# Moving a plan into the last attention turn, early expert weights ahead of their rows, and one hidden layer into the other PSUM ring

## The chip, the cores and the metric

The kernel runs on one core of a Trainium2 chip. The metric is device microseconds (us) of one execution; nine runs were timed, and one more execution was profiled. The engines are PE (matrix multiply; PEld is its weight load), DVE (vector), ACT (scalar, activations), POOL (GpSimd) and SP, which here only issues DMAs. In the views of the profile, L12 is line 12 of the kernel, and times in a timeline count from the start of the span.

## The reference

The reference is a gated cross attention followed by a gated mixture of eight experts, in float32. B is 8, 256 tokens per batch entry, width 128, 16 heads of 64, 8 experts with a hidden width of 512.

```python
q = layernorm(x) @ Wq + bq ; k = ctx @ Wk + bk ; v = ctx @ Wv + bv      # ctx is 8 x 1601 x 128
scores = q k^T / 8, causal mask of 256 x 1601 (key j is seen by query i when j <= i), -1e30 where masked
x = x + tanh(g_xattn) * (softmax(scores) v @ Wo + bo)
y = layernorm(x)
expert of a token = argmax(softmax(y @ Wr + br))
for i in range(8):
    xi = y * (expert == i)
    out = out + (relu(xi @ W1[i] + b1[i]) @ W2[i] + b2[i])
x = x + tanh(g_ffn) * out
```

A token that an expert does not own still goes through it as zeros, so each token gets its own expert's output plus a constant of the other seven.

## The kernel before

**Attention.** Batch entries are taken in four pairs, heads in eight pairs. A group g is one pair of heads of one pair of batch entries: 32 groups (NG), g = 0 to 31; b is the batch entry in the pair, and turn index i = 2b + j with j the head. The loop over g is software-pipelined: in turn g, PE makes the queries and keys of group g + 1, the scores of group g, the transposes (`turn`) of the probabilities of group g - 2, and its product with the values. DVE takes the row maximum (`scores`, L549 and L551) and copies the transposes out of PSUM (L605); ACT takes the exponentials (`exps`, L572); DVE takes a reciprocal (L586), and POOL multiplies the probabilities with it (L595, two instructions for each b).

**Routing.** After a pair's attention output and second layer norm, `router(p)` makes logits and each token's expert, `router_places(p)` its place in a store of rows sorted by expert (14 small matmuls and five DVE steps), and `scatter(n)` on POOL's queue writes 128 tokens' rows there by an indirect DMA. Pair 3, the last, is handled in two halves `a` and `b` (`class Half`), straight after the loop.

**Early chunks.** A chunk is 128 rows of one expert. Those that pairs 0 to 2 fill completely are known early: `plan_full` (18 small DVE steps; L1054 is the line that records all of them) finds up to five, NA = 5, and writes their numbers to `load_full`. SP loads each number (`fetch_number`, L941), and issues DMAs of the chunk's rows (132 KB, `fetch_rows`, L945) and of its expert's weights (578 KB, `fetch_weights`, L955) from a copy in DRAM named `later`. Each early chunk is then transposed (`turned_rows`), goes through `first_layer`, `hidden`, `second_layer` and `sums` in `last_routing`, in between the routing of half `b`. The other 18 chunks follow in `experts`: first the eight own ones, whose rows can be fetched only when the last scatter has landed.

**What sets the order.** The schedule is manual: each engine runs its instructions in the order in which the program states them. The order around the change is `last_turns`, where g = 30 and l = 31. There DVE has, in order: reciprocal (31,0), copies of turns (30,0) and (30,1), reciprocal (31,1), nine plan steps, copies of (31,0) and (31,1), the other nine, copies of (30,2) and (30,3). On SP's queue, `fetch_full` follows the plan. PE goes on with products for pair 3's output (`y_last0`, `y_last1`, L779), the residual (L774), and the halves' routing.

**PSUM.** Of eight banks, four hold scores, two are the ring `pt` of the transposes, two the ring `misc`. A tile takes a bank of its ring where it is first written in program order, and waits for the readers of the tile that had it. `hidden_bank` gives an early first layer a bank of `pt`; the ring there goes xs_0, hs_0, xs_2, hs_1, hs_2, so hs_1 takes the bank of hs_0.

Of the kernel before, what the change touches and what calls it, by code (L numbers as in the profile page):

```python
# [35 lines left out]
NA = 5  # L36
# [17 lines left out]
def tile_gated_xattn_moe(  # L54
# [19 lines left out]
    def misc(name):  # L74
        return ps_m.tile([P, 512], F32, tag="misc", name=name)
# [226 lines left out]
    _, first = counted("first", [E], [[N, E]])  # L302
    _, fills = counted("fills", [E, NFULL], [[0, E], [P, NFULL]], P)
# [175 lines left out]
    NG = NC * NPAIR  # L479
# [459 lines left out]
    def fetch_number(i):  # L939
        plan, j = ("full", i) if i < NA + E else ("rest", i - NA - E)  # L940
        number[i] = nc.sync.value_load(chunk_of[plan][0:1, j : j + 1], min_val=0, max_val=E * NT - 1)  # L941
# [18 lines left out]
        engine.tensor_tensor(r[:, D : 2 * D], r[:, D : 2 * D], v[:, AT_C : AT_C + D], ALU.add)  # L960

    def hidden_bank(i):
        if i < NA:
            return ps_t.tile([P, 512], F32, tag="pt", name=f"hs_{i}").unsqueeze(1)
        return ps_s.tile([P, 2, 512], F32, tag=f"sc{i % 2}", name=f"hs_{i}")
# [68 lines left out]
        nc.gpsimd.memset(warm[:, 0:1], 0.0)  # L1034

    def fetch_full():
        weights_behind = {1: (0,), 4: (1, 2, 3, 4)}
        for i in range(NA):
            fetch_number(i)
            fetch_rows(i)  # L1040
            for k in weights_behind.get(i, ()):
                fetch_weights(k)

    def last_turns(a):


        g, l = NG - 2, NG - 1
        b = Half(1, misc("y_last1")[:, 0:S], banks[0][:, 1, 0:S], banks[1][:, 1])
        steps = plan_full()

        def plan(n):
            for _ in range(min(n, len(steps))):
                f, *args = steps.pop(0)
                f(*args)  # L1054

        normalized(l, 0)
        turn(g, 0)
        turn(g, 1)
        exps(l, 1)
        scatter(10)  # L1060
        normalized(l, 1)
        scatter(11)
        apart()
        a.residual()
        a.out(NC - 4)
        plan(9)
        turn(l, 0)
        turn(l, 1)
        a.attend(g, nc.scalar)
        plan(len(steps))  # L1070
        fetch_full()
        a.out(NC - 3)
        turn(g, 2)
        turn(g, 3)
        a.attend(l, nc.scalar)
        a.out(NC - 2)
        b.out(0)
        b.residual()
        a.out(NC - 1)
        a.statistics()  # L1080
        a.deviation()
        turn(l, 2)
        turn(l, 3)
        a.turned()
        b.out(1, 2)
        a.logits()
        b.attend(g, nc.vector)
        a.normalized()
        a.choice()
        b.out(3)  # L1090
        b.attend(l, nc.scalar)
        a.apply()
        b.out(4, 5)
        a.places(cb[NPAIR - 2], cb[NPAIR - 1])
        a.scatter(0)
        b.out(6, 7)
        return a, b
# [85 lines left out]
    def beside_scores(p, c):  # L1183

        f, n = p - 1, p + 1
        outs = []
        if f >= 0:
            if p < NPAIR - 1:
                outs = [c - 2] if 2 <= c <= 5 else []
            else:  # L1190
                outs = [2 * c - 4, 2 * c - 3] if 2 <= c <= 3 else []
            if outs:
                attention_out(f, outs)
                for t in range(max(outs[0] - len(outs), 0), outs[0]):
                    norm2_stats(f, t)
            if c == (7 if p < NPAIR - 1 else 5):
                norm2_turn(f)
        if n < NPAIR:
            if c == 3:
                prologue_c(n)  # L1200
            if c == 5:
                prologue_x(n)
        if outs:
            evict_out(f, outs)
            if outs[-1] == 3:
                for t in outs:
                    norm2_stats(f, t)
                ln_scales(f"y{f}")
        if f == 1 and c == 0:
            router(0)  # L1210
        if f == 1 and c == 1:
            router_places(0)
        if f == 2 and c == 0:
            router(1)
        if f == 2 and c == 1:
            router_places(1)
        if f == 2 and c == 6:
            router_places(2)

    def beside_values(p, c):  # L1220

# [6 lines left out]
    with tc.manual_schedule():  # L1228
        plain_constants()
        for t in range(4):  # L1230
            ln_stats("x0", x_sb[0], t)
        ln_scales("x0")
        keep_awake(22)
        bias_vectors()
        prologue_c(0)
        keep_awake(3)
        prologue_apply(0)
        prologue_x(0)
        keep_awake(3)
        query(0)  # L1240
        masks = [step for p in range(NPAIR) for step in [mask_bias(p)] * 4]
        mask_steps = lambda n: [next(masks.pop(0)) for _ in range(n)]
        mask_steps(4)
        key(0, nc.vector)
        value(0)
        value(1, nc.vector)
        biases(0)
        scores(0, 0)
        exps(0, 0)
        mask_steps(4)  # L1250
        scores(0, 1)
        routing_constants()
        mean, rest_of = mean_value(), others()
        for g in range(NG):
            p, c = g // NC, g % NC
            old, new = g - 2 if g >= 2 else None, g + 1 if g + 1 < NG else None
            if g == 1:
                gates()
            if NC + 3 <= g < 2 * NC + 3:
                for i in range(2 * (g - NC - 3) + 1, min(2 * (g - NC - 3) + 3, NFILL)):  # L1260
                    fill(i)
            if p >= 1 and c == 2:
                residual(p - 1)
            if old is not None:
                turn(old, 0)
            if new is not None:
                query(new)
            if g == NC + 1:
                next(mean)
            if old is not None:  # L1270
                turn(old, 1)
            if g == NG - 1:

                o_old = misc(f"o_{old}")
                a = Half(0, misc("y_last0")[:, 0:S], banks[0][:, 0, 0:S], banks[1][:, 0])
                a.out(*range(NC - 4))
            if g > 1:
                exps(g - 1, 1, 0)
            if g > 0:
                beside_copies(p, c)  # L1280
            if NC - 4 <= g < NC:
                mask_steps(2)
            if new is not None:
                key(new)
            if g > 1:
                exps(g - 1, 1, 1)
            if g == 0:
                exps(0, 1)
            if old is not None:
                turn(old, 2)  # L1290
            if 1 <= g <= NG:
                for b in range(2):
                    normalized(g - 1, b)
            if p + 1 < NPAIR and c == 3:
                ln_scales(f"x{p + 1}")
            if g in (1, 2, 3, 5, 6):

                add_keys(g if g < 4 else g - 1)
            if g == 6:
                experts_weights()  # L1300
            if p < NPAIR and c == 4:
                add_bo(p)
            if g == NC - 1:
                join_keys()
            if g in (20, 21, 22, 24):
                next(rest_of)
            if g + 2 < NG:
                value(g + 2)
            if g == NC + 1:
                next(mean)  # L1310
            beside_values(p, c)
            if old is not None:
                turn(old, 3)
            if g == 3:
                router_constants()
            if g == 2:
                scaled()
            beside_scores(p, c)
            if g == 0:
                beside_copies(p, c)  # L1320
            if g == 1:
                routing_casts()
                more_constants()
            if g > 0:
                biases(g)
                scores(g, 0)
                exps(g, 0)
                scores(g, 1)
            if g == NC:
                next(mean)  # L1330
            if old is not None:
                values(old, o_old if g == NG - 1 else None)
            if g == NG - 3:
                router(2)
            if g == 0:
                add_keys(g)
            if NC + 4 <= g < NC + 4 + E:
                other(g - NC - 4)
            if 21 <= g < 28:
                next(rest_of)  # L1340
            if g == NC + 12 + E:
                keep_weights()
            if 20 <= g < 24:
                scatter(g - 20)
            if g == NG - 2:
                residual(NPAIR - 1)
            if 26 <= g:
                scatter(g - 22)
        last_routing(*last_turns(a))
        experts()  # L1350


# [31 lines left out]
```

## Time and profile before

| | us |
|---|---|
| median of 9 runs (lowest, highest) | 358.85 (357.04, 359.51) |
| the profiled execution | 358.12 |
| its span | 356.4 |
| PE busy | 333.9 (94%) |
| DVE busy | 245.4 (69%) |
| POOL busy | 216.3 (61%) |
| ACT busy | 208.0 (58%) |
| mean granted TensorE clock | 0.990 |

The page's slices show where the time lies: the attention loop to some 285 us, the last routing and the early chunks to 315, the expert chunks to 348, and the last stores. Busy time of PE is no proof of work at full speed: a matmul at half clock counts double. The granted clock is 1.0 for nearly the whole span; the stretches where it is not are the ones to look up. In the timeline views the columns are: start, us, engine, line, operation, written<-read, shapes, count, and in brackets the engine's idle time before it with what ended it. In sums over stretches: length, then busy time of PE, PEld, DVE, ACT and POOL with counts, granted clock, share of DMA, GB/s.

### The profile page before, as it was taken

Reading aid. Unit: us, or ns where it says so; the run is one execution under the profiler, and the core shown is the slowest. Engines: PE = TensorE matmul, PEld = TensorE weight load, DVE = VectorE, ACT = ScalarE, POOL = GpSimd, SP = SyncE. Lnnn points to the kernel's source line nnn. Section 1 sums busy time; section 2 is a strip of 40 time slices with the busy share of each in tenths; the row PEclk is TensorE's granted clock in tenths of the full one; section 3 lists DMA queues with packets and bytes.
Section 4 is the critical chain, followed back from the end, with each engine's and each line's share of the span. In section 5 each row is a group of like instructions: output and inputs, shape, how many; then the busy total and the mean of one; then the engine's idle time right before and its main releaser. Section 6 shows DMA issues by size and latency. Waiting matters only on the chain.

```text
span 356.4 us, 9265 instructions
## 1 busy us (share of the span) xinstructions
PE 333.9 (94%) x3244; PEld 236.1 (66%) x3244; DVE 245.4 (69%) x857; ACT 208.0 (58%) x743; POOL 216.3 (61%) x315
## 2 busy tenths in 40 slices
PE   7978999999999999999999999999999879889993
PEld 2435656667677766666766566677566657879993
DVE  3578889784777778787766887846787775654441
ACT  2277687765556757565565765745765712546651
POOL 6165675672365777769673566593775841717773
PEclk9999999999999999999999999999999989999997
DMA  6989775797899995000000000000390007659940
GB/s 206 275 140 202 116 107 86 110 325 220 235 386 383 386 384 184 2 2 2 3 2 15 17 18 16 2 2 15 151 404 30 30 32 230 234 161 345 399 152 16
DMA packets 36471, 53.69 MB, mean 151 GB/s; under 512 B 3945, under 2 KB 22973, under 8 KB 36424
## 3 DMA queue, kind: packets, MB, share of 16 engines
q1 hardware_dynamic: 28280, 44.00, 36.3%
q0 software_dynamic: 7360, 8.73, 12.9%
q8 instruction: 26, 0.43, 0.5%
q10 hardware_dynamic: 784, 0.36, 0.3%
q14 instruction: 21, 0.17, 0.1%
HBM read 27.82 MB, written 25.71 MB: 150 GB/s over the span
## 4 chain that ended last, share of the span: by engine, by line
PE 61%; DVE 14%; DMA 9%; ACT 6%; issue 3%; POOL 3%; ACTq 1%; SPq 1%; POOLq 0%; DVEq 0%
PE pt L603 8%; DMA rows<-in_ctx_dram 7%; PE k L491 7%; PE o L616 7%; PE y L660 6%; PE hs L986 6%; PE sc L541 5%; PE v L506 5%; PE ys L1002 5%; DVE sc L551 5%; PE q L484 4%; ACT prob L572 4%; PE y_last L779 2%; DVE nmax L549 2%; POOL prob L595 2%
## 5 line engine op out<-in xcount | busy, mean ns | idle before, releaser
L572 ACT ACTIVATE prob<-sc,nmax 128x129 f32<-128x129 f32 (+1 forms) x256 | 105.4, 426 | 89.1 <-DVE nmax L551 66.5
L595 POOL TENSOR_TENSOR prob<-prob,rs 128x256 f32<-128x256 f32 (+1 forms) x128 | 102.9, 863 | 60.2 <-DVE rs L586 58.7
L603 PEld LDWEIGHTS pt<-ident,prob 128*128 128x128 f32 x384 | 46.5, 141 | 55.4 <-issue 44.3
L605 DVE COPY probT<-pt 128x384 f32<-128x384 f32 x128 | 67.2, 545 | 11.7 <-PE pt L603 11.3
L603 PE MATMUL pt<-ident,prob 128*128 128x128 f32 x384 | 64.3, 278 | 3.8 <-DVE probT L605 2.2
L551 DVE CUSTOM_DVE_ANT_0 sc<-sc,bias 128x256 f32<-128x256 f32 x128 | 55.3, 432 | 4.5 <-DVE nmax L549 0.2
L572 ACT ACTIVATION_READ_ACCUMULATOR prob<-sc,nmax 128x1 f32 x256 | 53.7, 210 | 0.0
L616 PE MATMUL o<-probT,v 128*64 128x256 f32 x480 | 45.6, 332 | 0.0
L541 PE MATMUL sc<-kT,qT 64*64 64x256 f32 (+3 forms) x1024 | 41.9, 298 | 0.0
L616 PEld LDWEIGHTS o<-probT,v 128*64 128x64 f32 x480 | 29.7, 136 | 16.8 <-issue 7.0
L491 PE MATMUL k<-cT,arena 128*128 128x512 f32 x64 | 35.5, 636 | 2.6 <-DVE arena L634 1.6
L506 PE MATMUL v<-arena,cT 128*128 128x512 f32 x64 | 33.1, 601 | 1.7 <-ACT qT L486 1.6
L484 PE MATMUL q<-xT,arena 128*128 128x512 f32 x64 | 33.1, 598 | 0.1
L541 PEld LDWEIGHTS sc<-kT,qT 64*64 64x64 f32 x1024 | 31.6, 134 | 0.1
L549 DVE TENSOR_REDUCE nmax<-sc 128x2 f32<-128x258 f32 x64 | 26.9, 420 | 4.1 <-PE sc L541 3.8
L586 DVE RECIPROCAL rs<-ssum 128x4 f32<-128x4 f32 x64 | 11.1, 173 | 25.1 <-ACT prob L572 22.1
L1020 POOL DMA_INDIRECT out_dram<-o,rows x18 | 17.9, 996 | 15.7 <-DVE o L1013 11.5
L486 ACT ACTIVATE qT<-q,bqT 128x512 f32<-128x512 f32 x32 | 22.2, 694 | 7.8 <-PE q L484 7.3
L994 ACT ACTIVATE h<-hs,arena 128x128 f32<-128x128 f32 x60 | 17.1, 368 | 11.9 <-ACT h L994 9.7
L660 PE MATMUL y<-wo_sb,arena 128*128 128x128 f32 x192 | 23.3, 276 | 0.4 <-DVE zero L370 0.2
L497 ACT ACTIVATE kT<-k,bT 128x512 f32<-128x512 f32 x31 | 21.4, 692 | 2.5 <-PE k L491 2.2
L660 PEld LDWEIGHTS y<-wo_sb,arena 128*128 128x128 f32 x192 | 22.2, 192 | 0.9 <-DVE zero L370 0.9
(242 smaller groups left out, 506.7 us busy)
## 6 DMA issues: line engine op xcount, KB each, us to landing
store<-blank SPq DMA_DIRECT2D x16, 1056.0 KB, 14.7
arena<-later SPq DMA_DIRECT2D x15, 578.0 KB, 6.0
rows<-in_ctx_dram POOLq DMA_DIRECT2D x5, 1024.0 KB, 9.5
later<-ws SPq DMA_DIRECT2D x1, 4624.0 KB, 15.8
rows<-store SPq DMA_DIRECT2D x23, 132.0 KB, 2.3
ws<-in_L_ffn_W_dram SPq DMA_DIRECT2D x1, 2048.0 KB
ws<-in_L_ffn_W_dram SPq DMA_DIRECT2D x8, 256.0 KB, 3.7
rows<-in_ctx_dram SPq DMA_DIRECT2D x1, 1024.0 KB, 7.2
```

The costliest lines, as they stand in the source:

```text
L484: nc.tensor.matmul(ps, lhsT=wq_sb[:, c * P : (c + 1) * P], rhs=xT[p], start=True, stop=True)
L491: nc.tensor.matmul(ps, lhsT=wk_sb[:, c * P : (c + 1) * P], rhs=cT[p], start=True, stop=True)
L506: nc.tensor.matmul(ps, lhsT=cT[p][:, t * P : (t + 1) * P], rhs=wv_sb[:, c * P : c * P + 512], start=True, stop=True)
L541: nc.tensor.matmul(s[HB * u : HB * (u + 1), j, at : at + n], lhsT=q[r, lo : lo + HB], rhs=k[r, b * S : b * S + n], start=(t == 1), stop=True,)
L549: nc.vector.tensor_reduce(m[:, 0], s[:, :, U0:K1], AX.X, ALU.max, negate=True)
L551: nc.vector.tensor_tensor_reduce(out=s[:, j, K1:U1], in0=s[:, j, K1:U1], in1=bias[:, 2 * (g // NC) + b], scale=-1.0, scalar=-NEG_ALL, op0= ...
L572: nc.scalar.activation(pr[:, j, lo:hi], s[:, j, lo:hi], AF.Exp, bias=m[:, t, j : j + 1], scale=-1.0 if t else 1.0, accum_out=sm[:, t, j : ...
L595: nc.gpsimd.tensor_tensor(pr[:, :, lo:hi], pr[:, :, lo:hi], r, ALU.mult)
L603: nc.tensor.transpose(ps[:, n * P : (n + 1) * P], pr[:, j, K0 + n * P : K0 + (n + 1) * P], ident)
L605: nc.vector.tensor_copy(pt, ps[:, 0 : 3 * P])
L616: nc.tensor.matmul(o[DK * j : DK * (j + 1), n * P : S], lhsT=v[:, 2 * b + n, cols], rhs=probT[g, 2 * b + j][:, 0:S] if n == 0 else probT[g ...
L660: nc.tensor.matmul(ps[:, i * D : (i + 1) * D], lhsT=attT[p * NC + c][:, t * P : (t + 1) * P], rhs=wo_sb[:, c], start=(c == 0), stop=(c == ...
```

## The change

Five edits, made together:

- `router_places(2)` moves, in turn 30, from before the scores to after the values of group 28 (and so behind them on PE and DVE).
- `plan_full` is called in turn 31; its 18 steps are issued as 4 after turn (29,1), 3 after group 30's reciprocals, 3 in `last_turns` after reciprocal (31,0), and the last 8 before `fetch_full`.
- In `last_turns`, `normalized(l, 0)` moves behind `turn(g, 0)`, `turn(g, 1)` and `exps(l, 1)`.
- `fetch_full` issues the five numbers and weights first, and the five rows behind them.
- `hidden_bank(1)` takes a bank of `misc`.

```diff
     def hidden_bank(i):
+        if i == 1:
+            return misc("hs_1").unsqueeze(1)
         if i < NA:
             return ps_t.tile([P, 512], F32, tag="pt", name=f"hs_{i}").unsqueeze(1)
...
     def fetch_full():
-        weights_behind = {1: (0,), 4: (1, 2, 3, 4)}
+
         for i in range(NA):
             fetch_number(i)
+            fetch_weights(i)
+        for i in range(NA):
             fetch_rows(i)
-            for k in weights_behind.get(i, ()):
-                fetch_weights(k)
-
-    def last_turns(a):
+
+    def last_turns(a, plan):
...
-        steps = plan_full()
-
-        def plan(n):
-            for _ in range(min(n, len(steps))):
-                f, *args = steps.pop(0)
-                f(*args)
-
-        normalized(l, 0)
         turn(g, 0)
         turn(g, 1)
         exps(l, 1)
+        normalized(l, 0)
+        plan(3)
         scatter(10)
         normalized(l, 1)
         scatter(11)
         apart()
         a.residual()
         a.out(NC - 4)
-        plan(9)
         turn(l, 0)
         turn(l, 1)
         a.attend(g, nc.scalar)
-        plan(len(steps))
+        plan(18)
         fetch_full()
...
         if f == 2 and c == 1:
             router_places(1)
-        if f == 2 and c == 6:
-            router_places(2)
...
             if g == NG - 1:
+                full = plan_full()
+
+                def plan(n):
+                    for _ in range(min(n, len(full))):
+                        f, *args = full.pop(0)
+                        f(*args)
+
+                plan(4)
 
                 o_old = misc(f"o_{old}")
...
             if 1 <= g <= NG:
                 for b in range(2):
                     normalized(g - 1, b)
+            if g == NG - 1:
+                plan(3)
...
             if g == NG - 3:
                 router(2)
+            if g == NG - 2:
+                router_places(2)
...
-        last_routing(*last_turns(a))
+        last_routing(*last_turns(a, plan))
```

## The prediction

> **What bounds the kernel now.** I read the page first (PE busy 94% of the span), then the chain of waits through the last attention turns and the routing, then each engine's timeline there, SP's queue, and last the sums over the stretches of the granted clock. From 315.65 us on PE runs without a gap to 348 (the expert chunks), and the attention loop up to 270 us isn't touched. So the end moves by what moves the first own chunk, and the change is decided between 270 and 315 us.
>
> The chain of waits, start, us, what:
>
> ```profile
> 287.28 1.28 DVE wide_full L1054
> ...
> 289.23 0.48 DVE probT L605
> 289.70 0.04 issue
> 289.75 0.33 PE pt L603
> ...
> 305.96 1.16 PE hs L986 x8
> ...
> 312.81 2.02 DMA rows<-store
> ```
>
> The plan sits on the chain: copies of the last turns wait behind it on DVE, and PE behind the copies. Later the chain runs through the second early first layer to the own rows, which wait for the last scatter. The engines' timelines:
>
> ```profile
> 275.90 1.95 PE L779 MATMUL y_last<-wo_sb,arena 128*128 128x128 f32 x16
> 289.75 1.01 PE L603 MATMUL pt<-ident,prob 128*128 128x128 f32 x6 [1.82 <-DVE probT L605]
> 305.96 1.16 PE L986 MATMUL hs<-xsT,arena 128*128 128x128 f32 x8 [0.91 <-ACT h L994]
> ...
> 287.28 1.27 DVE L1054 TENSOR_TENSOR wide_full<-end_full,num_i 128x40 f32<-128x40 f32 x1
> 289.02 0.20 DVE L1054 TENSOR_TENSOR wide_full<-num_e,whose_full 128x40 f32<-128x40 f32 x1
> 286.87 1.61 POOL L595 TENSOR_TENSOR prob<-prob,rs 128x256 f32<-128x256 f32 x2
> 277.08 0.70 ACT L637 ACTIVATE arena<-o,bT 128x512 f32<-128x512 f32 x1
> ```
>
> To see: the same 128x40 step takes 0.20 us alone and 1.27 while POOL normalizes; it ends as POOL's second instruction does (288.48). SP's queue, and three granted-clock stretches (PE is the first busy column):
>
> ```profile
> 293.62 1.72 SPq L945 DMA_DIRECT2D rows<-store  x2
> 295.67 0.33 SPq L955 DMA_DIRECT2D arena<-later  x1
> 296.83 2.62 SPq L945 DMA_DIRECT2D rows<-store  x3
> 299.69 2.12 SPq L955 DMA_DIRECT2D arena<-later  x4
> ```
>
> ```profile
> 287.89:291.30 3.41, 1.59 (x15) 1.09 (x14) 3.13 (x13) 0.00 (x0) 1.74 (x3) 1.00 0.12 42
> 291.30:294.72 3.42, 3.42 (x18) 2.94 (x15) 1.34 (x5) 0.47 (x1) 0.00 (x0) 0.50 0.03 5
> 301.54:304.96 3.42, 2.69 (x21) 2.07 (x20) 1.45 (x10) 0.97 (x3) 2.29 (x5) 1.00 0.98 336
> ```
>
> After a stretch with 1.59 us of PE work the clock is 0.50 for the next 3.4 us; after one with 2.69 it isn't (nor after one with 1.76, early in the kernel).
>
> **Part 1: the third pair's places move behind group 30's scores.** Five DVE steps (273.06 to 273.98) leave the path ahead of the row maximum. That could start when its scores are done, 273.33 instead of 273.90 (at group 31 the maximum follows the scores' start by 0.83): 0.57 gained, and ACT's exponentials move with it: 275.48 to 274.91, the eviction L637 277.08 to 276.51, group 30's second exponentials end 278.83 instead of 279.40. The steps come back on DVE at 275.98 to 276.90 and PE's 14 small matmuls (0.43) after the values. The places' bank now comes after o_28's in the ring of two. In the trace y_last0 starts at 275.90, before L637 reads o_28 (277.08), so it stood in the places' bank; in the new order its turn is o_28's. I take that: a.out(0 to 3) waits for L637, 277.27. The other end: the places' bank, 276.95.
>
> **Part 2: plan in pieces.** Pitches are those of the plan's rows (18 steps from 286.02, less the held 1.05 and a pair of copies). DVE: copies of turns (29,0), (29,1) 276.90 to 277.90, plan(4) to 278.91. PE: a.out 277.27 to 279.06, turn (29,2), its copy 279.59 (before 278.22), reciprocals 280.06, and POOL's normalization of group 30 starts 0.33 later. plan(3): the reduce runs, wide_full is issued 0.5 after the reciprocal, inside POOL's first instruction (0.57 then 1.03 long), so I let it end with the second, as in the row shown: 282.05. Then one reduce, the copy of (29,3), and group 31's maximum starts at **282.8, before 280.31: 2.5 later**. Bounds: not held, 281.4; without the bank wait too, 280.8; held through all four of POOL's instructions, 284.3.
>
> From there by rows: both maxima 2.65; the two copies of group 30, now ahead of the reciprocal, 1.0; POOL's normalization 0.33 + 1.6, under which plan(3) is held at no cost but 0.3 (the next reciprocal waits for ACT anyway, 288.3); transposes and two copies of group 31, 1.47; then the first of the 8 steps left falls into POOL's next normalization (it starts 1.17 after the other's end, being behind scatter(10)) and ends with it, 2.77 after that end; the seven others 1.4. So load_full is ready 9.75 after the maximum: **292.55, before 291.79, 0.76 later**. Of 18 steps 10 leave the turn's end, and the gain goes into the wait for the maximum. PE does lose its 1.82 stall, but waits instead from 284.8 to 288.4 for the normalization; it would meet the slow clock one stretch earlier (as much work as before lies in it) and reach the early rows' turn at 301.7, as before (301.57).
>
> The Trainium skill speaks against this part: SBUF — State Buffer, "Who interferes with whom", says that a DVE instruction with two SBUF inputs contends with a GpSimd instruction that reads SBUF, and that the later one fully blocks until the first finishes. By that rule each hold ends with the instruction under way (287.50 in the trace), load_full is ready some 2 us earlier, and the sum would be 357.6. The row, which outlasts the next instruction too, decides.
>
> **Part 3: weights ahead of rows.** Before, rows 0 and 1 were issued 1.83 and 3.17 after load_full and landed 2.1 later, with five us to spare. Now SP issues: load and weights 0 at +1.3 (1.83 less the rows' own waits), then 1.15 each (1.145 for number and row), rows from +6.5. The queue keeps order: rows issued behind weights at 324 to 334 us took 4.9 to 5.5 us to land, alone 2.1. A row's fixed part is 2.1 less its 135 KB at 365 GB/s (what the DMA moved from 321 to 335 us), 1.75. So row 1 lands at 1.3 + 1.75 + (5 x 592 + 2 x 135) KB / 365 GB/s = 11.9 after load_full: **304.4**. (The same sum gives 307.9 for the last weights before; the trace has 308.0.) The early weights' gain is nothing: before, they were there before their layers. Behind the waiting transposes on PE stand the second half's transposes, its logits, first_layer(0): the path to the last scatter. From row 1 to the places' matmuls: 0.25 + 0.91 (transposes, ACT, to the logits) + 0.47 + 0.97 + 0.35 + 0.99 = 3.95, that is 308.4; before 306.95. So 1.4 later, with part 4 in it. DVE, POOL, the scatter's landing and the own rows keep their distance (306.95 to 314.96), PE's early chunks too (7.5 us to 314.47).
>
> PE then idles from 301.7 to 304.4. In the stretch 301.54 to 304.96 about 0.8 us of work is left, under the 1.59 that slowed it, so the clock is 0.50 to 308.4: of the 2.8 us of PE work ahead of the places the half lost is about 1.3. Sum: 1.4 + 1.3 = 2.7 later. The Trainium skill (TensorE: Matmul & The Clock Gate, "Why this matters for your kernels") puts the limit at gaps over some 3 us; by that rule this gap costs nothing and the sum is 1.4. The trace slowed after a 1.82 gap with thin work around it.
>
> **Part 4: hs_1 in the other ring.** y_last0 was read at 296, so the bank is free: the 0.91 wait for hidden(0) goes. ys_0 takes y_last1's bank, read by 302.7. Nothing is late; it's worth 0.9 at most, counted above.
>
> **Sum.** 358.1 (the profiled execution; span 356.4) + 2.7 = 360.8. The runs' median is 358.85, 0.7 above that execution, so I leave the sum as it is and let the range lean up.
>
> **Rivals.** (a) The rows come late but the clock doesn't drop: the stretches run free of the kernel's own order, and a boundary in the middle of the gap splits it. 359.5. For: 2.7 of 3.4 us; against: thin work on both sides. (b) Faster: POOL doesn't hold DVE, every moved step runs in its 0.2. Then the maximum is at 281.4, load_full at 281.4 + 2.65 + 1.0 + 1.95 + 1.45 + 1.55 = 290.0, row 1 at 301.9, PE waits 1.2 with no slow clock, the places come at 305.85: 1.1 earlier, **357.0**. It decides from load_full before 291.1 (306.95 - 15.85) on. For: big_full and tri_full, two inputs in SBUF, took 0.26 and 0.23 beside a scatter; against: wide_full at 1.27. (c) The hold ends an instruction sooner, or y_last0 keeps its bank with the slow clock missed: 357.4 to 359, within 0.3%. (d) The change doesn't do what it says: if rows overtook weights, they'd land near load_full + 9 and everything but parts 1 and 2 would vanish; the 5 us landings speak against it.
>
> **Chances.** The forecast 0.45 (its own range 359.9 to 361.8), (a) 0.15, (b) 0.17, (c) and (d) 0.23. A measurement tells 0.3% (1.1 us) from no change: faster 0.17, same 0.23, slower 0.60. The range runs from 357.3, a little over (b), to 362.3, the maximum held through all four instructions (1.5 more).
>
> **What would show it.** Right: y_last0 starts after L637; a 128x40 step of over 1 us just after group 30's reciprocals; group 31's maximum 2 to 2.5 later against group 30's scores; load_full at 292 to 293; xs waits 2 to 3 us for rows<-store, weights issued ahead; hs L986 has no wait for h; a clock of 0.50 in a stretch near 305. Wrong: load_full before 291, or xs not waiting.

## The result, and the profile after

| | before | after |
|---|---|---|
| median, us (runs) | 358.49 (46) | 363.53 (14) |
| lowest, highest | 356.42, 361.97 | 362.72, 365.87 |
| the profiled execution, us | 358.12 | 361.58 |
| its span, us | 356.4 | 359.9 |
| mean granted clock in it | 0.990 | 0.984 |

The ratio after to before is **1.0145, 95% interval 1.0126 to 1.0164**: 5 us slower. The forecast was 2.7 us slower, with a range that ended at 362.3. So the direction was right and the size was not.

Group 30's scores start at 272.75 us in the trace after and at 272.50 before; 0.25 is taken off where a time after is set against one before. Below, "the places" means the start of the last half's places matmuls (L716). The chain of waits after (start, us, what):

```profile
273.58 0.44 DVE nmax L549
...
280.79 0.62 DVE wide_full L1271
...
285.95 1.59 POOL prob L595 x2
287.58 1.33 PE pt L603 x5
...
299.31 5.53 DMA rows<-store
304.97 0.61 PE xs L979 x2
...
313.54 2.44 DMA store<-rows,posi_last
316.19 2.06 DMA rows<-store
```

The plan's long step is gone from the stretch where it stood, and what has come in is a transfer, the early chunks' rows, 5.53 us from their issue at 299.31 until PE can go on. The engines' timelines after show the wait and the plan's places:

```profile
277.53 2.05 PE L779 MATMUL y_last<-wo_sb,arena 128*128 128x128 f32 x16 [0.86 <-ACT arena L637]
286.59 0.33 PE L603 MATMUL pt<-ident,prob 128*128 128x128 f32 x1 [1.89 <-POOL prob L595]
304.97 0.61 PE L979 MATMUL xs<-ident,rows 128*128 128x128 f32 x2 [2.27 <-DMA rows<-store]
308.58 1.91 PE L988 MATMUL hs<-xsT,arena 128*128 128x128 f32 x8
310.29 0.24 PE L716 MATMUL sc<-hot_last,before 128*128 128x8 bf16 x2
...
280.79 0.61 DVE L1271 TENSOR_TENSOR wide_full<-end_full,num_i 128x40 f32<-128x40 f32 x1
282.01 0.42 DVE L549 TENSOR_REDUCE nmax<-sc 128x2 f32<-128x258 f32 x1
289.42 0.99 DVE L1271 TENSOR_TENSOR wide_full<-wide_full,end_full 128x40 f32<-128x40 f32 x1
291.74 0.17 DVE L1271 CAST load_full<-at_full 128x13 int32<-128x13 f32 x1
280.74 3.17 POOL L595 TENSOR_TENSOR prob<-prob,rs 128x256 f32<-128x256 f32 x4 [1.87 <-DVE rs L586]
```

xs is the transpose of the early rows. It waits 2.27 us on PE, and the last half's places, behind it, come at 310.29 where they came at 306.95. load_full, the early chunks' numbers, is ready at 291.91, 0.1 earlier than before once the 0.25 is taken off. SP's queue after, and the stretches of the granted clock (the columns as before):

```profile
293.26 5.70 SPq L955 DMA_DIRECT2D arena<-later  x5
299.31 3.01 SPq L945 DMA_DIRECT2D rows<-store  x5
```

```profile
286.98:290.39 3.41, 2.81 (x14) 1.77 (x14) 2.17 (x4) 0.53 (x3) 3.18 (x4) 0.50 0.13 43
290.39:293.81 3.42, 3.42 (x17) 2.71 (x18) 2.44 (x10) 0.47 (x1) 1.14 (x2) 0.50 0.11 41
...
304.05:307.46 3.41, 2.01 (x14) 1.64 (x15) 1.34 (x7) 0.38 (x1) 3.12 (x8) 1.00 0.59 206
307.46:310.87 3.41, 3.41 (x22) 3.35 (x22) 1.42 (x7) 2.23 (x8) 0.29 (x1) 0.50 0.09 32
310.87:314.29 3.42, 3.42 (x32) 3.42 (x32) 2.45 (x13) 1.95 (x8) 1.86 (x3) 1.00 0.11 40
```

All five weights are issued ahead of the rows. The clock is 0.50 in the stretch behind the gap, and in two stretches behind the 1.89 us wait for POOL as well; before it was 0.50 in one stretch of this part.

### The profile page after: what moved, and what is told of

Its sections match the earlier page's. It is cut to its first block, busy times and chain, and to the rows that moved or that the text cites. A ratio compares the mean times of both kernels' runs of the same rounds, so it can differ in the third digit from the quotient of the medians.

```text
span 359.9 us, 9261 instructions
## 1 busy us (share of the span) xinstructions
PE 337.8 (94%) x3244; PEld 238.5 (66%) x3244; DVE 246.3 (68%) x857; ACT 207.9 (58%) x743; POOL 216.3 (60%) x315
## 4 chain that ended last, share of the span: by engine, by line
PE 61%; DVE 17%; ACT 7%; DMA 6%; issue 4%; POOL 3%; SPq 1%; POOLq 0%; DVEq 0%; ACTq 0%
PE pt L603 8%; PE k L491 8%; PE o L616 6%; DVE sc L551 6%; PE v L506 6%; PE y L660 6%; PE sc L541 5%; ACT prob L572 5%; PE hs L988 4%; PE q L484 4%; PE ys L1004 4%; DVE nmax L549 2%; DMA rows<-store 2%; DVE arena L634 2%; PE sc L522 2%
## 5 line engine op out<-in xcount | busy, mean ns | idle before, releaser
L603 PEld LDWEIGHTS pt<-ident,prob 128*128 128x128 f32 x384 | 47.6, 143 | 54.0 <-issue 44.0
L603 PE MATMUL pt<-ident,prob 128*128 128x128 f32 x384 | 65.3, 282 | 2.9 <-POOL prob L595 2.6
```

Of the source, the lines that this page charges most:

```text
L603: nc.tensor.transpose(ps[:, n * P : (n + 1) * P], pr[:, j, K0 + n * P : K0 + (n + 1) * P], ident)
```

## The experiments

The theory after the result: the whole loss is part 3 (weights ahead of rows), through rows that land late and a clock that drops in the wait for them. Its rivals: the plan in pieces (parts 1 and 2) costs something too, or the lateness alone, without the clock, makes the loss.

Each timed run lists its mean granted clock. In the stretches of the traces the clock is 1.0 or 0.50, so the time that a run spent at half clock is 2 x span x (1 - clock). That view of the runs is used further down.

**Undo part 3 alone.** The changed kernel with the old order on SP's queue:

```diff
     def fetch_full():
-
+        weights_behind = {1: (0,), 4: (1, 2, 3, 4)}
         for i in range(NA):
             fetch_number(i)
-            fetch_weights(i)
-        for i in range(NA):
             fetch_rows(i)
+            for k in weights_behind.get(i, ()):
+                fetch_weights(k)
```

> The changed kernel with the early rows issued as before (rows 0 and 1, weights 0, rows 2 to 4, weights 1 to 4); the plan in pieces and hs_1 stay. Late-rows theory (rows behind 2.96 MB of weights keep PE waiting, then a slow clock): the wait of xs for rows<-store goes, PE comes to it some 0.75 us later than before because of the plan, hs_1 gives back up to 0.9, so about the time of the kernel before, 357.5 to 359.5. Rival (the plan's pieces hold group 31's maximum and slow the clock for two stretches, and that is the loss): 361.5 to 363.5, nearly all of it stays.

Measured: 0.9998 [0.9963, 1.0034], 358.85 us against 358.87. xs waits for nothing, and the places come 33.17 us after the start of group 30's scores (34.45 before, 37.54 after). Without part 3 nothing is lost.

**Part 3 alone**, the reverse edit made in the kernel before:

> The kernel before with one part alone: five numbers and weights issued ahead of five rows. Late-rows theory: xs waits till about load_full + 13, 305 us, instead of 301.6; with the slow clock after it 4 to 5 us later, 362 to 363.5. Rival (the plan's pieces are the loss): the rows land late but mostly under other work, under 360.

Measured: 1.0201 [1.0129, 1.0273], 366.26 us, nearly 3 us above the expected 362 to 363.5. The PE timeline of this run:

```profile
306.86 0.81 PE L977 MATMUL xs<-ident,rows 128*128 128x128 f32 x2 [3.09 <-DMA rows<-store]
...
312.79 2.08 PE L986 MATMUL hs<-xsT,arena 128*128 128x128 f32 x8 [0.65 <-DVE xsT L979]
```

From load_full to xs it takes 13.0 us, as in the trace after (13.05), and the eight matmuls of hs take 2.08 us at half clock where they take 1.16 at the full one. Part 3 by itself makes the whole loss. Whether it makes more without the other parts isn't shown: the interval overlaps those of the changed kernel.

**Parts 1 and 2 alone**: the first edit above, and hidden_bank as it was:

```diff
     def hidden_bank(i):
-        if i == 1:
-            return misc("hs_1").unsqueeze(1)
```

> The kernel before with the third pair's places moved, the plan in pieces and the later normalization, without the weights ahead and without hs_1. Late-rows theory: PE comes to the early rows' transposes 0.5 to 1 us later, 358.5 to 359.7. Rival (the plan's pieces are the loss): 361.5 to 363.5, with two stretches of half clock from 287 us on the path.

Measured: 1.0007 [0.9974, 1.0040]. The replanned turn is worth nothing that can be told from zero, either way.

**The changed kernel again**, beside these three on one chip:

> The changed kernel again, for a second profile: its profiled execution took 361.6 us, two under the runs' median. If the place of the granted-clock stretches makes that difference, the half-clock stretch near 305 to 309 will lie elsewhere and the time from xs to the last scatter will be 1 to 2 us longer; if the rows' landing makes it, xs will wait longer for rows<-store, with the same clock. Both: median 363 to 364.

Measured: 1.0178 [1.0109, 1.0247], 364.54 us. Its PE timeline and its stretches:

```profile
305.18 1.04 PE L979 MATMUL xs<-ident,rows 128*128 128x128 f32 x2 [5.66 <-DMA rows<-store]
...
312.19 0.24 PE L716 MATMUL sc<-hot_last,before 128*128 128x8 bf16 x2
```

```profile
303.45:306.86 3.41, 1.35 (x4) 0.68 (x4) 0.58 (x3) 0.17 (x1) 1.20 (x4) 0.50 0.78 287
306.86:310.28 3.42, 3.16 (x15) 3.16 (x16) 1.23 (x7) 0.40 (x2) 0.00 (x0) 0.50 0.02 5
310.28:313.69 3.41, 3.41 (x21) 3.35 (x21) 1.33 (x6) 2.85 (x10) 0.00 (x0) 0.50 0.00 0
313.69:317.10 3.41, 3.41 (x33) 3.41 (x33) 2.36 (x9) 1.34 (x5) 2.77 (x7) 1.00 0.16 57
```

In this execution the clock did not drop early, PE reached the gap sooner and waited 5.66 us, and the clock was then 0.50 for three stretches, through all that leads to the last scatter. From xs to the places it takes 7.0 us, against 5.3 in the first profile. So one profile of this kernel doesn't stand for its runs: the forecast's single slow stretch is the mildest of those profiled.

**Keep PE's clock up through the gap.** 24 matmuls of ones, into a bank that is free there, stand in PE's program ahead of xs (keep_awake is a helper of the kernel that makes such matmuls):

```diff
         a.scatter(1)
+        keep_awake(24)
         turned_rows(e[:2], True)
```

> The changed kernel with 24 matmuls of ones (5.1 us at full clock, results unused) on PE ahead of the early rows' transposes, where PE waits for rows<-store. Theory (late rows cost about 2.5 us, and the clock that drops in the gap for one to three stretches of 3.41 us costs the rest): xs starts as late as before, 305, but the granted clock stays 1.0 from there, the last half's places follow xs by 4.0 to 4.5 us instead of 5.3 to 7.0, and the time is 360 to 361.8. Rival (the lateness alone, or the order on ACT and POOL behind it, makes the loss): places follow as late as before, 363 to 364.5, or later by the matmuls' own time.

Measured: 1.0104 [1.0012, 1.0196], 369.96 us against 365.91 (this chip runs the kernel before 2% slower than the others did). The clock is 1.0 in the profile until the last stores, xs to places takes 3.99 us, and xs still follows load_full by 13.3. The kernel is still 4 us slower than the one before, more than the expectation allowed. How much of the loss is gone can't be told here, as the changed kernel itself wasn't run on this chip.

**Three weights ahead instead of five**, the other two behind the rows:

```diff
         for i in range(NA):
             fetch_number(i)
-            fetch_weights(i)
+            if i < 3:
+                fetch_weights(i)
         for i in range(NA):
             fetch_rows(i)
+        for i in range(3, NA):
+            fetch_weights(i)
```

> The changed kernel with three early weights ahead of the rows instead of five, the other two behind them. Late-rows theory: row 1 lands 1.6 us earlier per weight taken away, about load_full + 10, 301.7; PE comes there at 299.5 to 302.5, so the wait is 0 to 2 us and the time 358.5 to 361. Rival (each weight ahead of the rows costs the same, whatever PE does): three fifths of the loss, 361.5 to 362.

Measured: 1.0024 [0.9985, 1.0062]. xs follows load_full by 9.84 us and waits 0.41. With two transfers of 578 KB fewer ahead of them, the rows land 3.2 to 4.3 us sooner (9.84 against 13.0 to 14.1) and use up PE's spare time, but little more. That is the price of the order as a function of its size: none ahead, and five us are spare; three, and they are gone; five, and the kernel loses 5.

**Is the earlier clock drop worth removing?** Eight matmuls of ones fill the idle time of PE in `last_turns`, in the first experiment's kernel and in the kernel before (the helper is the same in both):

```diff
+    def fill_pe(bank, n):
+        for _ in range(n):
+            nc.tensor.matmul(bank, lhsT=ones_bf, rhs=ones_bf[:, 0:1].to_broadcast([P, 512]), start=True, stop=True)
...
         a.out(NC - 4)
+        fill_pe(banks[0][:, 1], 8)
         turn(l, 0)
```

```diff
         a.out(NC - 3)
+        fill_pe(banks[1][:, 1], 8)
         turn(g, 2)
```

> The kernel of e1 (plan in pieces, hs_1, rows first) with 8 matmuls of ones (1.7 us) on PE ahead of turn (31,0), where it waits for POOL's normalization. Clock theory: the half-clock stretch from about 288 goes and PE comes to the early rows 1 to 1.5 us earlier: 357.2 to 358.2. Rival (copies and scatters set the path there, not PE): as e1, 358.5 to 359.2.

> The kernel before with 8 matmuls of ones (1.7 us) on PE ahead of turn (30,2), in its 1.82 us stall behind the plan. Clock theory: the half-clock stretch from 291 goes, 1 to 1.5 us earlier: 357 to 358. Rival (the 1.82 us stall isn't what drops the clock): the stretch stays, 358.5 to 359.2.

Measured: 1.0004 [0.9970, 1.0039] and 0.9993 [0.9956, 1.0031]. Neither profile has a half-clock stretch in this part, and the places come 31.99 and 32.84 us after the scores (34.45 before), but the layers then wait 1.6 and 1.9 us for their weights. The gain that both expectations named doesn't show in the times.

**The same again on another chip**, where the kernel before takes 358.67 us: the changed kernel, it with the 24 matmuls, and the two with eight:

> The changed kernel on the same chip as the three that follow, since the chip of e5 to e8 took 2% longer for the kernel before (its last 18 chunks took 43 us instead of 35). 1.3 to 1.8% over the kernel before, with a gap of 2 to 6 us ahead of xs and 7 to 10 us of half clock.

> The kernel of e5 (24 matmuls of ones in the gap). In e5 the clock stayed 1.0, and places followed xs by 4.0 us, but the end was 3.7 us over the kernel before on a chip whose last chunks wait for weights. Clock theory: here 2 to 3 us under e9 and 2.5 to 3.5 over the kernel before (the rows' lateness of 3.6, less the 0.9 of hs_1). Rival (clock without effect): as e9.

> The kernel of e7. In e7 the half-clock stretch was gone and places came 32.0 us after group 30's scores, in e1 33.2, in the kernel before 34.5; the end didn't move on that chip. If the weights of the last chunks hid it there: 1 to 2 us under the kernel before here, 356.5 to 358. Rival (something between places and the end takes it back on any chip): within 0.3%.

> The kernel of e8. There the half-clock stretch was gone and places came 32.8 after group 30's scores instead of 34.5. 1 to 1.5 us under the kernel before here, if the last chunks' weights hid it there; rival: within 0.3%.

Measured: 1.0141 [1.0078, 1.0203]; 1.0105 [1.0049, 1.0160]; 0.9998 [0.9961, 1.0035]; 0.9981 [0.9950, 1.0012]. The second gains 1 us on the first where 2 to 3 were expected, and the two intervals overlap. Its profile misses its aim in part: an early clock drop made PE late, so that the 24 matmuls ended after the rows had landed, and xs waited for PE itself. The third again waits for weights, 1.8 us. The fourth doesn't, and still its time isn't below the kernel before by more than the interval. Its first own chunk comes 40.77 us after the scores, against 42.46 in the profile before, and from that chunk the span goes on for 41.4 us in both. What differs is the baseline: the profile before has 7.1 us at half clock, the runs of that kernel on this chip 3.4 on the mean. So most runs before have little of that drop to lose; this is an argument from the listed clocks, not a separate run.

**The lateness by itself.** Both fillings in the changed kernel (eight before turn (31,0), 24 before xs), so that the clock stays up:

> The changed kernel with 8 matmuls of ones ahead of turn (31,0) and 24 ahead of the early rows' transposes, so that the clock drops nowhere in the stage and PE comes to the late rows at the same point in each run. Theory (lateness of the rows 2 us in the sum with hs_1, the clock 2.7 to 3.3): first own chunk 44.3 to 44.8 us after group 30's scores (before 42.5, changed 45.6 to 47.9), 360.3 to 361.3 in time. Rival (the clock's share was the matmuls' luck in e5): 363 and more.

Measured: 1.0089 [1.0062, 1.0115], 362.5 us against 359.4. The interval ends below that of the changed kernel (1.0126 to 1.0164), so filling PE's waits took off part of the loss. The expectation of 360.3 to 361.3 is missed. The PE timeline:

```profile
300.38 5.39 PE L213 MATMUL awake<-ones_bf 128*128 128x512 bf16 x23
306.77 0.77 PE L979 MATMUL xs<-ident,rows 128*128 128x128 f32 x2 [1.00 <-DMA rows<-store]
...
310.89 0.19 PE L716 MATMUL sc<-hot_last,before 128*128 128x8 bf16 x2
```

The clock is 1.0 until the last stores, xs to places is 4.1 us (the forecast had 3.95), and still 3.1 us are lost. From load_full to xs it takes 14.1 us here. So lateness is the larger part of the loss, and more than twice its forecast.

**hs_1 alone**, in the kernel before (the hidden_bank edit, taken from the change):

> The kernel before with hs_1 in the other ring alone. The 0.91 us wait of hs L986 for h goes: first own chunk up to 0.9 earlier against group 30's scores, 41.6 to 42.5, time 357.7 to 358.7. Rival (the last half's places wait for its choice, not for first_layer(1)): 0 to 0.2 us.

Measured: 0.9986 [0.9967, 1.0005]. Its profile has no clock drop ahead of the last stores, and the places come 0.7 us earlier against the scores than in the awake kernel before, the one with the eight matmuls (32.16 against 32.83), where hs still waits 0.91 for h. The wait is gone, and the first own chunk doesn't follow (40.85 against 40.77): the last scatter takes 3.08 us to land where it took 2.44.

**Why not: what a faster PE runs into.** The awake kernel before with hs_1, and then the same with a mixed order (rows 0 and 1; weights 0 to 2; rows 2 to 4; weights 3 and 4), in the kernel before and in the one with the change's plan:

```diff
     def fetch_full():
-        weights_behind = {1: (0,), 4: (1, 2, 3, 4)}
-        for i in range(NA):
+        for i in range(2):
             fetch_number(i)
             fetch_rows(i)
-            for k in weights_behind.get(i, ()):
-                fetch_weights(k)
+        fetch_weights(0)
+        fetch_weights(1)
+        fetch_number(2)
+        fetch_weights(2)
+        fetch_rows(2)
+        for i in range(3, NA):
+            fetch_number(i)
+            fetch_rows(i)
+        for i in range(3, NA):
+            fetch_weights(i)
```

> The kernel before with 8 matmuls of ones in the 1.82 us stall (e8, e12) and hs_1 in the other ring: the version that should beat both. 1.0 to 1.7 from the clock and 0.5 to 0.9 from hs_1: first own chunk 40.2 to 41 us after group 30's scores, time 356.3 to 357.6. Rival (what the path loses there is taken back by the last scatter or the chunks' weights): within 0.3% of the kernel before.

> The kernel of e15 with the early issues in the order rows 0 and 1, weights 0 to 2, rows 2 to 4, weights 3 and 4. In e15 PE had gained 1.4 us by the last half's places and then waited 1.5 us for weights 2 and 0.2 for others. Theory (weights behind rows 2 to 4 are the next bound): the wait of hs for arena<-later goes, first own chunk 40.3 to 41 us after group 30's scores, 0.8 to 1.5 us under the kernel before. Rival (the last scatter and the own rows bind anyway): within 0.3%.

> The kernel of e7 (plan in pieces, hs_1, 8 matmuls of ones ahead of turn (31,0)) with the same mixed order of issues. In e7 and e11 hs waited 1.6 and 1.8 us for arena<-later. Theory: that wait goes, first own chunk 40 to 40.8 us after group 30's scores (e11: 40.9), 1.0 to 2.0 us under the kernel before. Rival: within 0.3%, the own rows bind.

Measured: 0.9993 [0.9975, 1.0012]; 1.0006 [0.9978, 1.0034]; 1.0019 [0.9989, 1.0048]. None gains, as the rivals had it. The PE timeline of the first, the awake kernel before with hs_1:

```profile
308.32 1.13 PE L988 MATMUL hs<-xsT,arena 128*128 128x128 f32 x8 [1.52 <-DMA arena<-later]
```

And that of the second, with the mixed order:

```profile
305.67 0.30 PE L979 MATMUL xs<-ident,rows 128*128 128x128 f32 x1 [0.48 <-DMA rows<-store]
306.33 0.68 PE L979 MATMUL xs<-ident,rows 128*128 128x128 f32 x2 [0.36 <-DMA rows<-store]
...
315.79 0.30 PE L979 MATMUL hs<-ident,rows 128*128 128x128 f32 x1 [0.53 <-DMA rows<-store]
```

With the old order a PE that comes to xs 1.6 us earlier (27.46 after the scores, 29.07 before) waits 1.52 for the third layer's weights. With the mixed one that wait is gone, and PE waits for rows 2 to 4 instead, and then for the own rows. What is bought at one place on SP's queue is paid at the next. No kernel tried is faster than the one before by more than its interval; 0.9981 [0.9950, 1.0012] and 0.9986 [0.9967, 1.0005] come nearest.

**The time at half clock over the runs.** From each run's listed clock and span, for seven of the kernels, means in us; the last column is the mean time of the kernel less that of the kernel before in the same comparison:

```
kernel                            half clock   half clock, before   time less before
weights first alone                     18.6                  3.9                7.2
changed, beside it                      13.4                  3.9                5.9
changed, third time                     12.1                  3.4                5.1
changed, 24 matmuls                      7.6                  3.4                4.0
changed, 24 matmuls, slower chip         5.9                  4.4                3.7
changed, both fillings                   1.8                  4.4                3.0
rows first                               6.4                  3.9               -0.1
```

Inside 108 runs of the kernel before in five comparisons (one more, of 662 us, is left out), each us at half clock goes with 0.27 us more of time (standard error 0.04). Inside the 24 runs of the changed kernel it is 0.38 (0.12). At 0.27 the loss splits as follows. Both fillings: 3.0 + 2.6 x 0.27 = 3.7 us of lateness at equal clock. The changed kernel, third time: 8.7 us more at half clock, 2.3 us; 2.7 of 5.1 are left for the lateness. So, as an estimate, lateness is 2.7 to 3.7 us of the loss and the clock the rest, some 1.3 to 2.3. The price is a correlation among runs of one program, and the listed clock doesn't say where in the span it was low: at the very end, where PE idles (352.74 to 356.16 before), half clock costs nothing. It is a rough price, and no experiment set the clock alone, so the split is argued and not shown.

## Why the prediction was right in direction and wrong in size

**What bounds it, and where it is decided.** Right: between 270 and 315 us, by what moves the first own chunk. From the places to that chunk it takes 8.0 us before and 8.1 after (310.29 to 318.38).

**Part 1** was right to the hundredth. Group 30's maximum is at 273.58 (forecast 273.33, plus 0.25), and y_last0, in o_28's bank, starts at 277.53 behind L637 (277.27 plus 0.25).

**Part 2** had the mechanism and not the length of the hold. "I let it end with the second, as in the row shown" was the step that failed: wide_full took 0.61 us and ended with POOL's first instruction, so group 31's maximum came 1.45 later against the scores, not 2.5. PE's stall was exchanged for a wait for POOL's normalization, as forecast; it ended at 287.58, not 288.4, with the earlier maximum. The Trainium skill (SBUF — State Buffer, "Who interferes with whom") has the later instruction blocked until the first finishes; in the trace after that was right and the reading from the row wrong: the step at 289.42, issued 0.11 us after the second instruction of POOL's pair starts, also ends with that one. load_full was 0.1 earlier instead of 0.76 later. It didn't decide: parts 1 and 2 alone measure 1.0007. By the page's rule load_full would have been some 2 us earlier than the forecast; it was 0.9 earlier, and the sum of 357.6 fell with part 3, whose terms it shared.

**Part 3** had the mechanism and both sizes too small; here the forecast failed. The first mis-sized term is "1.3 + 1.75 + (5 x 592 + 2 x 135) KB / 365 GB/s = 11.9 after load_full": measured, up to xs, 13.0 to 14.1 in the six profiles with five weights ahead in which PE waited for the rows. In the profile after it didn't show, by luck: load_full 0.9 earlier than forecast took off most of the 1.15 more, and xs started at 304.72 (less 0.25) against the forecast's 304.4. The sums over single microseconds after show why:

```profile
294.00:295.00 1.00, 1.00 (x12) 0.95 (x9) 0.00 (x0) 0.47 (x1) 0.00 (x0) 1.00 0.69 162
295.00:296.00 1.00, 1.00 (x9) 0.95 (x9) 0.00 (x0) 0.00 (x0) 0.00 (x0) 1.00 1.03 416
...
298.00:299.00 1.00, 1.00 (x12) 0.67 (x11) 0.16 (x1) 0.00 (x0) 0.41 (x1) 1.00 0.65 157
299.00:300.00 1.00, 1.00 (x10) 0.79 (x10) 0.87 (x5) 0.00 (x0) 0.00 (x0) 1.00 1.02 277
...
302.00:303.00 1.00, 0.70 (x7) 0.51 (x5) 0.56 (x4) 0.26 (x1) 0.00 (x0) 1.00 0.97 393
```

The last column is GB/s. From 294 to 305 the eleven entries (162, 416, 249, 351, 157, 277, 301, 412, 393, 389, 379) have a mean of 317, not 365. The same 3230 KB at 317 take 10.2 us instead of 8.85: 1.3 more, about what is missing in this trace (13.05 less 11.9). The 365 came from a stretch in which the queue had long been full; the trace of before shows 336 over 301.54 to 304.96, which was in front of me. The rows were issued 7.4 us after load_full, not 6.5, behind weights at 1.2 to 1.7 us apart. Whether that or something else makes the rate dip at 298 was not tried.

The other half of the lateness is the baseline. The forecast took the places of the profile before, 306.95, and that profile has a half-clock stretch at 291.30 that costs it 1.6 us by the places (34.45 from the scores, 32.83 in the awake kernel before). After the change PE waits for the rows whether it came early or late, so what a run without that stretch gains before is lost after. 13.3 after load_full at 291.67, and 3.95 more, is 308.9; against 306.95 that is 2.0, and against 305.3 it is 3.6, beside the 3.7 at equal clock.

The second mis-sized term is the clock: "0.50 to 308.4 ... about 1.3", one stretch. The drop came as the row of the forecast said, after a gap of 2.27 us with thin work. The Trainium skill (TensorE: Matmul & The Clock Gate, "Why this matters for your kernels") puts the limit at some 3 us; gaps of 1.82 us (before), 1.88 (rows first) and 2.27 (after) each had a half-clock stretch that began 1.5 to 2.5 us behind them, so 3 us is no safe limit here. Nor does a gap of that length always bring one: hs_1 alone has the same 1.82 us gap at 289.13, and its clock stayed at 1.0. What may make the difference is where the gap lies. In every trace with several stretches they start on one grid of 3.41 us (before at 291.30 and 352.74, 18 steps apart; after at 286.98, 307.46 and 358.66, 6 and 15), at another place in each execution. Before, one step of the grid held the whole gap, with 1.59 us of PE work; in hs_1 alone, by the grid counted back from its last stretch, two steps shared it, with 2.01 and 3.00. Work alone is no sharp rule: 2.01 us in the step from 304.05 after did bring a drop, 1.53 in the second profile of the changed kernel did not.

What failed is that it would last one stretch: it lasted one, two and three in the three profiles of the changed kernel (3.41, 6.83 and 10.24 us behind the gap), and the loss over runs is 1.3 to 2.3 by the estimate above. The rows shown go with a reason: behind a half-clock step that PE's work filled (3.41 us) the clock was 1.0 again, from 310.87 in the first profile and from 313.69 in the second; behind one with 1.35, 2.81 or 3.16 us it stayed at 0.50.

**The level.** The forecast's sum was made on the profiled execution, 358.12. The profiled execution after is 361.58, 3.5 more, 0.8 above the forecast of 2.7; the median after lies 1.95 above that execution and the median before 0.4 above its own. So leaving "the sum as it is" was a step that failed too: the part that differs from run to run, the clock behind the gap, is the part that the change adds.

**Part 4** was right: hs at 308.58 waits for nothing, and it is worth no more than the 0.9 (0.14% by itself, its interval reaching 0.05% to the other side).

**The rivals.** (a) and (b) fell: the clock did drop behind the gap in all three profiles of the changed kernel, and load_full at 291.7 was not before 291.1. What (a) said of the stretches, that they run free of the kernel's own order, fits the grid above. (c) is half true, the hold did end an instruction sooner, yet the time wasn't 357.4 to 359. (d) fell: with five weights ahead xs came 13.0 or more after load_full, not 9, and fewer weights ahead brought the rows sooner.

## What to carry to other kernels

A small load that someone soon waits for shouldn't stand behind large ones on a queue, however early the large ones would then be; count the bytes ahead of it at the rate seen while the queue fills, and compare with the slack of the engine that waits. Measure the slack in a run without its own disturbance: a baseline that lost time to the clock hides how little slack there is. And where a change opens a gap in PE's work, price the slow clock behind it over several runs: one profile shows one draw.

## What the runs showed of the hardware that was not expected

How long a DVE step with two SBUF inputs was held beside POOL went with where in POOL's instruction it was issued. These rows are of the first experiment (the changed kernel with the old order of loads):

```profile
280.64 0.61 DVE L1271 TENSOR_TENSOR wide_full<-end_full,num_i 128x40 f32<-128x40 f32 x1
288.85 1.41 DVE L1271 TENSOR_TENSOR wide_full<-wide_full,end_full 128x40 f32<-128x40 f32 x1
...
280.59 3.16 POOL L595 TENSOR_TENSOR prob<-prob,rs 128x256 f32<-128x256 f32 x4 [1.88 <-DVE rs L586]
288.58 1.61 POOL L595 TENSOR_TENSOR prob<-prob,rs 128x256 f32<-128x256 f32 x2
```

Issued 0.05 us after POOL's first instruction starts, the step is let go when that one ends (0.61). Issued 0.27 after the start, it is held through the next one too: to 290.26, POOL's pair ending at 290.19. In the trace before it was issued 0.41 after the start and held for 1.27. So the rule cited under part 2 fits some rows and not these two; why isn't settled.

Ahead of the last stores the half-clock stretches come in multiples of 3.41 us (3.41, 6.83, 10.24). Eight matmuls of ones, 1.9 us, in PE's idle time in `last_turns` left all eight profiles that had them without one between 280 and 318 us; their timed runs still list some time at half clock, 1.8 to 7.1 us on the mean. In these experiments one chip took 365.9 us for the kernel before where the others took 358.7 to 359.4; its last 18 chunks took 43 us instead of 35, with waits ahead of first layers of 6.9 us in all (0.8 in the profile before), whose cause the trace doesn't name.
